# Spacing GpSimd's gathers and ranking a list-scheduled four-layer kernel anew

## The chip, the cores and the metric

The kernel runs on one core of a Trainium2 chip. A core has five engines that run beside each other, each with its own instruction queue in order: TensorE (PE, matmuls; its weight loads are listed as PEld), VectorE (DVE), ScalarE (ACT), GpSimd (POOL) and SyncE (SP, which here only issues DMAs). They meet through semaphores. The metric is the device time of one execution in microseconds (us): the median over the runs.

## What is computed

The input x is 8 sequences of 256 tokens with 128 features, in fp32. Four layers follow, each with a cross-attention to a context of 8 x 64 tokens and a feed-forward part, both added to x with a learned gate tanh(g):

```
for l in 0..3:
    x = x + tanh(g_xattn[l]) * xattn_l(layernorm(x), ctx)
    x = x + tanh(g_ffn[l])   * ffn_l(layernorm(x))
```

What bears on the change:

- Layer 0's feed-forward part is a mixture of experts: a base expert for every token, and for each token the two best of eight experts (128 -> 2 x 352 -> 128, SiLU gate), weighted by their softmax scores.
- Layer 1 has an attention of 16 heads over own tokens and context, and a dense mixture of eight small experts. Layer 2 has an attention of 16 heads over context, and a mixture of attention and feed-forward experts, gated by cosine similarities (the small tensors sims and sgate).
- Layer 3's feed-forward part quantises its weights to three values, w_q = clip(round(W / s), -1, 1) * s with s the mean of |W| of a row, and uses W + (w_q - W). It has one shared expert and the single best of eight experts for each token (128 -> 256 -> 128).

## The kernel before

**Tiles and stages.** The 2,048 tokens are 16 tiles of 128, in four chunks of four. x stays in SBUF. Matmuls run in fp32; "ps" in the profile is any PSUM bank, and rA, rC, rG, rK, rU and rF are regions of SBUF that many tiles share.

**The two routed mixtures.** Layer 0 and layer 3 send tokens to experts through DRAM. The normalised tokens are stored (xkd, zd), the routing makes index lists (d0idx, d30idx, d31idx), and each expert tile of 128 tokens is fetched by an indirect DMA that GpSimd issues (`gather`, L1151). PE transposes it (L888), multiplies it with its expert's weights (layer 0: L1263, L1282, L1288; layer 3: L2217, L2233, with L888 between), an evacuation copies it out of PSUM (L1301, L2245) and SP stores two tiles at a time (ygd by L1302, yd by L2246). Then the tokens fetch their experts' rows back, again by `gather` (index lists d0rows, d30rows, d31rows), and DVE adds them to x (L1312, L2252). There are 117 gathers: 39 of xkd, 32 of ygd, 19 and 11 of zd (layer 3 routes its first three chunks, then its last one), 12 and 4 of yd. SP stores the output two tiles at a time after L2252 (L2254).

**Other lines that the text touches.** `base_expert` (L1228, L1234) and `l3_shared` (L2193, L2197) are matmuls without routing, used as filler. L1512 are the scores of layer 1's attention, whose row maxima DVE takes (L1490); their operands come through a DMA rU<-rC (L1465, L1466) after L1458 and L1461. L1798 to L1805 prepare layer 2's gating from sims and sgate; L1800 is its matmul on PE, L1804 a step on ACT and L1805 one on DVE. L1826 is a matmul of layer 2's gating. L868 is the power function of the norms, on GpSimd. `l3_quantised` (L2120 to L2137) quantises two weight tensors in thirds: DVE makes two comparisons (L2129, L2130) and GpSimd four elementwise steps over 768 columns (L2131 to L2134).

**What sets the order.** The program isn't written in its order of execution. Each operation is recorded as a `Node` with a modelled cost and latency, its dependencies and a rank; `Plan.schedule` is a list scheduler over the five queues. At each step it takes, for each engine, the ready nodes that could start within a small slack of the earliest, and of these the one with the lowest rank; `emit` then writes each engine's instructions by planned start. The ranks come from the table RANKS: pairs of a node number and a rank, valid up to the next pair.

```
for (first, rank), (end, _) in zip(RANKS, RANKS[1:] + [(len(nodes), 0)]):
    for n in nodes[first:end]:
        n.rank = (rank, n.seq)
```

Where the plan has PE active for too small a share of the last 3.4 us (WINDOW, ENOUGH, LEAST), `fill` puts in dummy matmuls (bf16, 128x512, listed at L2298), whose results nobody reads. 31 small loads of constants for the later layers (L754, L993 to L1010, held back by `plan.hold`) are issued by SP among the stores of ygd. A gather is modelled at 1,250 ns of GpSimd and 1,300 ns more until it has landed.

Of the kernel before, what the change touches and what calls it, by code (L numbers as in the profile page):

```python
# [14 lines left out]
BF16 = mybir.dt.bfloat16  # L15
AF = mybir.ActivationFunctionType
ALU = mybir.AluOpType
AX = mybir.AxisListType

P = 128  # L20
# [67 lines left out]
class Node:  # L88
    __slots__ = (
        "seq", "rank", "calls", "cost", "lat", "deps", "kids", "wait", "ready", "table", "allocs", "uses", "line",  # L90
        "start", "eng", "end", "outs", "act",
    )


# [1 line left out]
SEM = 60.0  # L96


class Plan:
# [52 lines left out]
    def add(self, calls, items, cost, lat):  # L152
        n = Node()
# [15 lines left out]
        n.line = self.line()  # L169
        n.ready, n.start = self.hold, None  # L170
        n.act = sum(i[7] for i in items)
        n.outs = [x for i in items for x in i[1] if eng != "PE" and not isinstance(x, View)]
        for _, writes, reads, *_ in items:
            for x in reads:
# [67 lines left out]
    def schedule(self, square):  # L242
# [120 lines left out]
                    best = (t2, t, i)  # L363
            return best and best[1:]

        order = []
        todo = len(nodes)
        while todo:
            pick = None
            for e in ENGINES:  # L370
# [6 lines left out]
                for n in pool:  # L377
                    t = n.ready if n.ready > t0 else t0
                    if n.allocs:
                        ok, taken = True, []  # L380
                        for b in n.allocs:
                            pl = place(b, taken)
                            if pl is None:
                                ok = False
                                break
                            taken += range(pl[1], pl[1] + b.n)
                            if pl[0] > t:
                                t = pl[0]
                        if not ok:
                            continue  # L390
                    if e == "ACT" and n.table and n.table != table:
                        t += switch
                        if t - n.ready < PATIENCE:
                            t += 0.5 * switch
                    cand.append((t, n))
                    if t < low:
                        low = t
# [37 lines left out]
            for b in n.allocs:  # L435
                t1, i = place(b)
                t = max(t, t1)
                b.place = i
                kinds[b.kind] = kinds.get(b.kind, 0) + 1
                for j in range(i, i + b.n):  # L440
                    held[j] = b
                    spans[j].append([t, 1e18])
            n.eng, n.start = e, t
            free[e] = t + n.cost[e]
            lat = n.lat[e]
# [9 lines left out]
            else:  # L455
                x = next((x for x in n.outs if whole(x)), None)
                if x is not None:
                    heapq.heappush(steps, (n.end + SEM, n.seq, x))
                if begin is None and any(x.tensor.name == square.tensor.name for x in n.outs) and n.rank[1] > first_square:
                    begin = n.end + SEM  # L460
# [17 lines left out]
        order.sort(key=lambda n: (n.start, n.seq))  # L478
        self.order = order
        return order  # L480

    def dummy(self, j, weights, src):
        dst = self.psum[:, j * BANK : (j + 1) * BANK]
# [19 lines left out]


RANKS = [
    (0, -8.81423), (24, -3.9207), (39, 6.38523), (63, 5.89215), (87, 7.63505), (111, 8.13897), (135, 3.08915),
    (159, 5.79217), (183, 6.34169), (195, 2.37592), (219, 9.35483), (226, 7.73129), (239, 8.47319), (263, 9.41623),
    (287, 9.81073), (311, 9.81017), (335, 5.75831), (359, 7.11937), (383, 4.51516), (400, 12.473), (424, 11.4516),
    (448, 12.1111), (468, 10.9153), (492, 11.2491), (516, 13.9731), (527, 6.24473), (551, 4.81591), (575, 7.74998),
    (599, 9.83805), (623, 10.6955), (647, 5.78046), (671, 8.27812), (695, 4.60363), (719, -8.92199), (743, 3.38467),  # L510
    (767, 6.96523), (791, 3.62384), (815, 8.51202), (839, 1.56555), (863, 3.79945), (887, 6.97792), (911, 4.33277),
    (935, 8.78708), (943, 15.012), (951, 18.2171), (959, 16.913), (967, 10.4794), (975, 16.9253), (983, 9.99517),
    (991, 1.54625), (1015, 5.87219), (1039, 2.6703), (1063, -8.68786), (1087, 3.14673), (1096, 2.80187),
    (1120, 12.4378), (1144, 12.1551), (1153, 5.7225), (1177, 15.0894), (1183, 3.58836), (1193, 3.96122),
    (1217, 7.19124), (1241, 9.01458), (1250, 7.91182), (1274, 6.93102), (1280, 3.99039), (1290, 10.8385),
    (1314, 6.31445), (1338, 6.65857), (1354, 8.48851), (1378, 6.31126), (1402, 7.9314), (1411, 5.32165),
    (1435, 15.3732), (1441, -9.12596), (1451, -3.81797), (1475, -3.69121), (1499, 10.91), (1508, 15.3376),
    (1532, 13.6412), (1538, 9.82436), (1548, 4.51756), (1572, -4.85316), (1596, 11.2096), (1612, -3.99823),
    (1636, -3.026), (1660, 7.32202), (1669, 7.95703), (1693, 3.94619), (1699, 4.59663), (1709, 3.44889),
    (1733, 6.59853), (1757, 3.60586), (1766, 7.56498), (1790, 7.68471), (1796, 4.3326), (1806, 4.34554),  # L520
    (1830, 7.2283), (1854, 6.25525), (1870, 6.2584), (1894, 3.02858), (1918, 5.98574), (1937, 0.60987),
    (1961, 5.27954), (1982, 7.71269), (2006, 6.25101), (2030, 6.28834), (2046, 3.90444), (2070, 7.80619),
    (2094, 3.7545), (2118, 7.69472), (2142, 2.38528), (2145, 5.92942), (2169, 14.3495), (2193, 12.8278),
    (2208, 9.51468), (2232, 7.76875), (2256, -5.45801), (2271, 7.76656), (2295, 3.46247), (2319, 11.5164),
    (2334, 3.67181), (2358, -3.29604), (2382, 10.5902), (2397, 7.49049), (2421, 4.17373), (2445, 3.04442),
    (2460, -4.97886), (2484, -5.98313), (2508, 8.79012), (2523, 10.2729), (2547, -3.86213), (2571, 9.48064),
    (2586, 2.69215), (2610, 17.1353), (2634, 7.61745), (2649, -8.8357), (2655, 9.73474), (2676, 5.59728),
    (2700, 5.47862), (2707, 13.687), (2731, 10.4051), (2755, 10.1074), (2779, 7.67358), (2782, 4.52856),
    (2806, 5.49354), (2830, -9.18087), (2844, 8.0594), (2868, 8.15882), (2892, -9.18314), (2906, 7.30903),
    (2930, 3.85602), (2954, 4.00223), (2968, 4.2028), (2992, 12.5164), (3016, 15.0752), (3030, 9.25522),  # L530
    (3054, -9.20446), (3078, -3.75919), (3079, 5.5021), (3103, -8.64894), (3127, 5.41648), (3128, -9.10233),
    (3145, -9.09852), (3169, 10.0369), (3193, 3.34345), (3202, 6.24005), (3226, 4.85186), (3250, 3.79496),
    (3251, 3.12274), (3268, 2.65504), (3292, 5.52079), (3316, 8.04174), (3325, 6.36822), (3349, 12.6744),
    (3359, 17.8309), (3376, -8.71613), (3400, 14.6489), (3424, 6.97596), (3433, 7.31619), (3457, 1.40941),
    (3467, 1.92845), (3491, 10.0564), (3501, 6.76292), (3525, -4.75416), (3549, 3.12448), (3551, 2.78523),
    (3575, 1.25688), (3599, 5.04665), (3601, 14.9022), (3625, 11.1661), (3649, 6.38291), (3651, 11.7678),
    (3675, 7.02337), (3699, 4.12325), (3723, 10.4855), (3747, 14.702), (3762, 10.4015), (3786, 9.45812),
    (3810, 9.48594), (3811, 4.91636), (3828, 1.98819), (3852, 6.07668), (3876, 5.16349), (3885, 7.16907),
    (3909, 4.32541), (3919, 1.29563), (3943, 4.76685), (3967, 5.94095), (3969, 4.27357), (3993, 5.06055),
    (4017, 10.113), (4035, 10.3702), (4059, 17.4385), (4071, 8.68884), (4095, 17.3361), (4119, 4.54227),  # L540
    (4143, 8.44501), (4167, 6.73715), (4191, 7.19744), (4215, 7.46141), (4225, 7.86594), (4249, 9.71193),
    (4273, 8.26746), (4297, 12.837), (4315, -3.41036), (4339, 3.89787), (4345, 5.15199),
]


WINDOW, DUMMY, GUARD, ENOUGH, LEAST = 3400.0, 216.0, 150.0, 0.62, 0.48


def whole(x):
# [60 lines left out]
class Engine:  # L610
# [5 lines left out]
    def __getattr__(self, name):  # L616
        plan, eng = self.plan, self.eng

        def call(*args, **kw):
# [16 lines left out]
            elif eng == "POOL":  # L636
                c, lat = cost_pool(name, allargs, out, ins), 100.0
                if name == "indirect_dma_start":
                    c, lat = 1250.0, 1300.0
                    ins = [x for x in (kw["in_"],) if is_ap(x)]  # L640
                    for k in ("in_offset", "out_offset"):
                        if kw.get(k) is not None:
# [65 lines left out]
def tile_flamingo(ctx: ExitStack, tc: tile.TileContext, a: dict, out: bass.AP, n_sub: int = 8):  # L708
# [9 lines left out]
    def mk(shape, name, dtype=F32):  # L718
        return const.tile(shape, dtype, tag=name, name=name)

    regions = {k: mk([P, n], "r" + k) for k, n in (("A", 9792), ("G", 8192), ("U", 8192), ("K", 6144), ("C", 8960), ("F", 2048))}

    def put(region, at, shape, n=1):
# [1391 lines left out]
    def l3_quantised():  # L2115
        for i, (groups, size) in enumerate(((18, D), (9, 2 * D))):
# [9 lines left out]
            for k in range(3):  # L2126
# [1 line left out]
                q, lo = (z.rearrange("p (r l) -> p r l", l=size) for z in (bq_, bl_))  # L2128
                v.tensor_tensor(q, w[:, r], over(th[:, 0, r], size), ALU.is_gt)  # L2129
                v.tensor_tensor(lo, w[:, r], over(th[:, 1, r], size), ALU.is_lt)  # L2130
                g.tensor_tensor(q, q, lo, ALU.subtract)  # L2131
                g.tensor_tensor(q, q, over(sc[:, r], size), ALU.mult)
                g.tensor_tensor(q, q, w[:, r], ALU.subtract)
                g.tensor_tensor(q, q, w[:, r], ALU.add)  # L2134
                qf = bq_.rearrange("p (n l) -> p n l", l=P)
                for k3 in range(2):
                    evac(w3t[:, i, 6 * k + 3 * k3 : 6 * k + 3 * k3 + 3, :], turned(qf[:, 3 * k3 : 3 * k3 + 3], 3))  # L2137
# [234 lines left out]
```

## Time and profile before

| | us |
|---|---|
| median of 9 runs | 969.83 |
| lowest and highest | 968.21 and 973.93 |
| the profiled execution | 973.31 |
| its span in the trace | 971.1 |
| PE, DVE, ACT, POOL busy | 913.7, 684.6, 382.6, 299.0 |

A row of the profile's groups names line, engine, operation, output<-input and count; behind the first bar stand the busy time and the mean ns of one, behind the second the engine's idle time ahead of these instructions and what ended it ("<-DVE rstd L865" is a wait for DVE's result of line 865; "issue" is a wait that the profile can't name). The granted clock (PEclk) is the share of TensorE's full speed: 1 or 0.5 at any moment of this trace, means over a stretch lie between.

### The profile page before, as it was taken

How to read it: one execution, taken by the hardware profiler on the slowest of the kernel's cores; microseconds unless marked ns; L12 is line 12 of the kernel's file. 1: busy time of each engine (PE TensorE's matmuls, PEld its weight loads, DVE VectorE, ACT ScalarE, POOL GpSimd, SP SyncE). 2: the span in 40 equal slices, each digit the busy share in tenths (PEclk: the TensorE clock that was granted, in tenths of full speed). 3: DMA queues.
4: the chain of work that ended last, by engine and by line, in shares of the span. 5: the costliest groups of instructions: out<-in, count | busy, mean ns of one | idle time of the engine just before them, and what ended most of it. 6: DMA issues, size and time to landing. Idle time of an engine off the chain costs nothing. (4 is left out here: it accounts for less than half of the span.)

```text
span 971.1 us, 18385 instructions
## 1 busy us (share of the span) xinstructions
PE 913.7 (94%) x6669; PEld 613.0 (63%) x6669; DVE 684.6 (70%) x2059; ACT 382.6 (39%) x1096; POOL 299.0 (31%) x320
## 2 busy tenths in 40 slices
PE   8999799999999999999999899989999999999983
PEld 4646587755554464455677677557775768867872
DVE  7885355569776766774866799867579768697642
ACT  2242223214445436346756877101134044044631
POOL 6406530266110010101311234330125741213464
PEclk9999999979999999999999999989999999999997
DMA  8412421121000000000102000210000000000353
GB/s 267 131 54 72 104 45 36 37 66 35 19 15 10 14 10 10 11 2 23 45 1 72 1 18 23 52 25 1 1 2 0 2 1 12 12 12 20 67 87 90
DMA packets 55781, 36.50 MB, mean 38 GB/s; under 512 B 14898, under 2 KB 52027, under 8 KB 55692
## 3 DMA queue, kind: packets, MB, share of 16 engines
q1 hardware_dynamic: 47724, 25.56, 9.4%
q0 software_dynamic: 3744, 7.68, 4.2%
q10 hardware_dynamic: 4224, 2.10, 0.7%
q8 instruction: 54, 0.88, 0.4%
q14 instruction: 35, 0.29, 0.1%
HBM read 25.08 MB, written 7.67 MB: 34 GB/s over the span
## 5 line engine op out<-in xcount | busy, mean ns | idle before, releaser
L868 POOL TENSOR_TENSOR rstd<-rstd,mhalf 128x4 f32<-128x4 f32 (+2 forms) x44 | 44.5, 1013 | 298.5 <-DVE rstd L865 256.5
L1490 DVE TENSOR_REDUCE nmx<-ps 128x2 f32<-128x640 f32 x128 | 100.2, 818 | 17.6 <-PE ps L1512 16.3
L1512 PE MATMUL ps<-rU 32*128 32x256 f32 (+1 forms) x1024 | 104.9, 445 | 5.1 <-DMA rU<-rC 2.1
L1521 ACT ACTIVATE rA<-ps 128x1024 f32<-128x1024 f32 x64 | 65.1, 1023 | 75.3 <-PE ps L1512 71.6
L1909 PE MATMUL ps<-rK,rG 128*128 128x128 f32 x768 | 90.3, 276 | 0.0
L1909 PEld LDWEIGHTS ps<-rK,rG 128*128 128x128 f32 x768 | 88.0, 192 | 3.3 <-issue 2.8
L1512 PEld LDWEIGHTS ps<-rU 32*128 32x128 f32 (+1 forms) x1024 | 56.4, 187 | 48.8 <-DVE nmx L1490 22.4
L1736 ACT ACTIVATE rA<-ps,nm 128x64 f32<-128x64 f32 x256 | 75.9, 348 | 10.2 <-DVE nm L1732 7.8
L1901 PE MATMUL ps<-rG,rK 128*128 128x512 f32 x128 | 60.8, 624 | 0.0
L1736 ACT ACTIVATION_READ_ACCUMULATOR rA<-ps,nm 128x1 f32 x256 | 60.7, 242 | 0.0
L1263 PE MATMUL ps<-rA,rC 128*128 x156 | 52.6, 467 | 0.0
L1151 POOL DMA_INDIRECT rC<-xkd,d0idx x39 | 37.3, 955 | 35.0 <-PE ps L888 21.0
L1901 PEld LDWEIGHTS ps<-rG,rK 128*128 128x128 f32 x128 | 25.1, 203 | 27.8 <-issue 27.0
L1895 DVE TENSOR_TENSOR rG<-rC,ps 128x512 f32<-128x512 f32 x64 | 40.4, 678 | 0.0
L1557 PE MATMUL ps<-rA 128*9 128x256 f32 (+1 forms) x512 | 37.0, 385 | 0.5 <-ACT rA L1521 0.4
L1151 POOL DMA_INDIRECT rC<-ygd,d0rows x32 | 31.7, 992 | 13.8 <-issue 7.2
L1263 PEld LDWEIGHTS ps<-rA,rC 128*128 128x128 f32 x156 | 27.6, 194 | 10.4 <-ACT rC L1258 0.5
L1288 PEld LDWEIGHTS ps<-rA,rU 128*128 128x128 f32 (+1 forms) x234 | 30.4, 195 | 3.4
L1721 PE MATMUL ps<-rG,rA 128*128 128x512 f32 x64 | 31.1, 604 | 1.0 <-DVE rA L1753 0.6
L1758 PE MATMUL ps<-rU,rA 128*128 128x128 f32 x256 | 31.9, 278 | 0.0
L1288 PE MATMUL ps<-rA,rU 128*128 (+1 forms) x234 | 31.8, 279 | 0.0
L1758 PEld LDWEIGHTS ps<-rU,rA 128*128 128x128 f32 x256 | 30.1, 192 | 2.1 <-issue 1.3
(523 smaller groups left out, 2062.2 us busy)
## 6 DMA issues: line engine op xcount, KB each, us to landing
rA<-in_L_ffn_exp_wgu_dram SPq DMA_DIRECT2D x4, 704.0 KB
ygd<-rC SPq DMA_DIRECT2D x19, 128.0 KB
rK<-in_L_xattn_Wkv_dram SPq DMA_DIRECT2D x2, 1024.0 KB
rU<-rC SPq DMA_DIRECT2D x64, 32.0 KB
yd<-rG SPq DMA_DIRECT2D x14, 128.0 KB
x<-in_x_dram SPq DMA_DIRECT2D x4, 256.0 KB
rA<-in_L_ffn_exp_wd_dram SPq DMA_DIRECT2D x2, 512.0 KB
xkd<-rC ACTq DMA_DIRECT2D x4, 256.0 KB
```

The lines of the kernel that those rows point to most:

```text
L868: power(r[:, 0 : n * len(kinds)], n * len(kinds))
L1151: g.indirect_dma_start(out=dst, out_offset=None, in_=src, in_offset=bass.IndirectOffsetOnAxis(ap=idx, axis=0))
L1263: with together():
L1288: with together():
L1490: v.tensor_reduce(nmx_of[b][:, qt, h0 : h0 + 2], sc[:, :, 0:KEYS], AX.X, ALU.max, negate=True)
L1512: with together(cost=640.0 if bm is not None else 500.0):
L1521: s.activation(e, st, AF.Exp)
L1736: with together():
L1758: with together(cost=2280.0):
L1895: v.tensor_tensor(xe[:, 2 * i + k, :], src, pgs[:, k, :], ALU.mult)
L1901: with together():
L1909: with together():
```

## The change

Three edits.

First, a gather node is marked, and the scheduler lets a gather start only 5,000 ns (in the plan's time) after the third-last one. If it was held up by that, `after` puts a tiny copy ahead of it on GpSimd: it copies one column of the newest finished result of an engine other than GpSimd (as the plan sees it) into a scratch column, so that at run time GpSimd waits for that step before it issues the gather.

```
+        n.gather = n.lat.get("POOL") == GATHER
...
+                    if n.gather and len(gathers) > 2 and gathers[-3] + GATHERS > t:
+                        t = gathers[-3] + GATHERS
...
+            if n.gather:
+                if len(gathers) > 2 and gathers[-3] + GATHERS >= t and ended:
+                    self.after(n, max((c for c in ended if c[0] <= t), default=None))
+                gathers.append(t)
...
+                    if e != "POOL":
+                        ended.append((n.end + SEM, n.seq, x))
...
+    def after(self, n, mark):
+
+        if mark is None:
+            return
+        x = mark[2]
+        while len(x.shape) > 2:
+            x = x[:, 0]
+        x, dst = x[:, 0:1], self.scratch
+        if x.dtype == BF16:
+            dst = dst.bitcast(BF16)[:, 0:1]
+        n.calls["POOL"].insert(0, lambda e, fix: e.tensor_copy(dst, x))
...
+GATHER, GATHERS = 1300.0, 5000.0
```

Second, the four GpSimd steps of the quantisation work on halves of each group of columns, in a loop over the halves:

```
-                g.tensor_tensor(q, q, lo, ALU.subtract)
-                g.tensor_tensor(q, q, over(sc[:, r], size), ALU.mult)
-                g.tensor_tensor(q, q, w[:, r], ALU.subtract)
-                g.tensor_tensor(q, q, w[:, r], ALU.add)
+                for h in (slice(0, size // 2), slice(size // 2, size)):
+                    qh, wh = q[:, :, h], w[:, r, h]
+                    g.tensor_tensor(qh, qh, lo[:, :, h], ALU.subtract)
+                    g.tensor_tensor(qh, qh, over(sc[:, r], size // 2), ALU.mult)
+                    g.tensor_tensor(qh, qh, wh, ALU.subtract)
+                    g.tensor_tensor(qh, qh, wh, ALU.add)
```

Third, the table RANKS is replaced as a whole: ranges of up to 24 nodes become ranges of up to 16, and nearly every value differs.

```
 RANKS = [
-    (0, -8.81423), (24, -3.9207), (39, 6.38523), (63, 5.89215), (87, 7.63505), (111, 8.13897), (135, 3.08915),
...
+    (0, -10.4081), (16, -5.43032), (24, -10.1179), (39, -4.23222), (55, -3.9187), (63, 1.22023), (79, 15.8053),
...
```

Counted in the instruction orders of the two programs: PE's real matmuls are the same in number and shape, in another order, and its dummies are 125 before and 123 after. GpSimd has 87 tiny copies and 24 halves more. 14 PSUM evacuations of 128x256 go from DVE to ACT. SP issues the same 276 DMAs, in another order: eight of the constants (sims, one sgate, layer 2's norms) come first among them, and the stores of the output come earlier among those of yd.

## The prediction

> **What bounds the kernel now.** I read the page's busy times and its slices first, to see which engine sets the pace.
>
> ```profile
> PE 913.7 (94%) x6669; PEld 613.0 (63%) x6669; DVE 684.6 (70%) x2059; ACT 382.6 (39%) x1096; POOL 299.0 (31%) x320
> ...
> PE   8999799999999999999999899989999999999983
> ...
> PEclk9999999979999999999999999989999999999997
> ```
>
> TensorE (PE) sets it: 913.7 of 971.1 us busy, so all its idle time together is 57.4 us. GpSimd (POOL), on which every part of the change sits, is busy for 299.0 us. It can cost time only where PE waits for it. Next I read a table by stage.
>
> ```profile
> 0.00:27.00 27.00, 23.74 (x103) 12.90 (x103) 21.48 (x99) 6.55 (x15) 15.86 (x29) 0.94 0.89 273
> ...
> 100.00:125.00 25.00, 17.67 (x94) 13.86 (x93) 9.02 (x28) 5.26 (x14) 11.86 (x14) 0.88 0.41 95
> ...
> 200.00:225.00 25.00, 22.88 (x111) 12.20 (x110) 18.54 (x38) 3.44 (x11) 13.74 (x15) 0.80 0.22 57
> ...
> 930.00:971.10 41.10, 23.25 (x139) 18.58 (x137) 13.31 (x35) 9.31 (x24) 19.98 (x21) 0.81 0.45 92
> ```
>
> The columns are the stretch, its length, busy us (and instructions) of PE, weight loads, DVE, ACT and POOL, then the granted clock and the DMAs. Subtract PE's busy time from the length: 3.3 us of idle time lie in the first stretch, 7.3 in 100 to 125, 2.1 in 200 to 225, 17.9 in the last one. Together that is 30.6 of the 57.4; the rest is strewn in waits below 1.5 us, except one of 3.3 us at 603. So the change can be worth much only in three places: the stall near 115, the entry into the first attention near 205, and the tail.
>
> **Part 1: PE's own work.** The instruction orders of the two programs hold the same real matmuls; the planned dummies (L2298) go from 125 to 123. One takes 0.38 us, so -0.7 us. They also move: 24 to 50 in layer 1's attention, 31 to 18 in layer 2, 70 to 55 elsewhere. Moved at equal number they cost nothing by themselves. That the planner wants as many as before also says that it sees about as much room on PE as before.
>
> **Part 2: the stall near 115.** The waits of PE in 100 to 125 are one line.
>
> ```profile
> PE ps L1800 <- DVE tk_simsq L1798: 7.3, 1, 7.3
> ```
>
> Behind it lies SyncE's queue: 31 small loads of constants are issued from 106.14 to 122.4, about 0.5 us each, behind the fourth store of ygd, which waits for its tile. The 25th (the second sgate) is seen by ACT's L1804 at 123.49, 17.4 us after the first issue. The new order puts sims and seven more loads first, but DVE now meets this block two tiles earlier, and still passes through L1805, which needs the 25th load. Counting PE's rows, the fourth ygd store is ready 2.7 us later, and PE reaches the block 6.2 us later. The stall would run from 114.1 + 6.2 = 120.3 to 123.5 + 2.7 + 0.5 (ACT, DVE) = 126.7: 6.4 us in place of 7.3, so I take -0.9. Bounds: -7.3 (gone) and +2.7 (all of the later store).
>
> **Part 3: the entry into the first attention.** Here 32 gathers of ygd follow the last store of ygd; four of them, two norms and a transfer rU<-rC lead to the first scores (L1512).
>
> ```profile
> 206.00 0.81 PE L1512 MATMUL ps<-rU 29*128 29x320 f32 x4 [2.12 <-DMA rU<-rC]
> ...
> 209.95 4.87 PE L1512 MATMUL ps<-rU 29*128 29x320 f32 x20
> ...
> 218.71 1.70 PE L1512 MATMUL ps<-rU 29*128 29x320 f32 x12
> ```
>
> Two things are to be seen: PE waited 2.12 us for the chain, and afterwards the same matmul took 244 ns (4.87 over 20) where it later took 142. The granted clock was 0.5 from 207 to 217. Pricing the slow rows against their fast forms gives 2.0 (L1512), 1.1 (L1458 and L1461, 2.28 against 1.18) and 1.1 (L1228, 2.08 against 1.02): 4.2 us in all. In the new order only three gathers go at once; the fourth waits for a DVE step behind the first. PE's filler before L1512 is equal, some 21 us, so the delay is seen. One pitch of a gather is 1.25 us (0.95 and 0.30 between two): +1.3, bounds 0 (the filler hides it) and +4 (a landing of 2.5 us and 1.5 of DVE come between). The slow clock I leave as it is, since the wait ahead of it does not shrink.
>
> The Trainium skill, "TensorE: Matmul & The Clock Gate", Part 1: The HAM clock gate, says that the clock falls to half after an idle window of about 3.4 us. Here 2.12 us of idle time was followed by 0.5, so the row is stricter than the rule. By the rule the stretch could vanish with slightly denser work and the sum would be 4.2 us lower; by the row it stays.
>
> **Part 4: paced gathers and tiny copies.**
>
> ```profile
> L1151 POOL DMA_INDIRECT rC<-xkd,d0idx x39 | 37.3, 955 | 35.0 <-PE ps L888 21.0 <-issue 4.9 <-DVE d0idx L1139 4.5
> ...
> L2133 POOL TENSOR_TENSOR rA<-rA,rU 128x768 f32<-128x768 f32 x6 | 12.8, 2138 | 0.5
> ...
> L1974 POOL COPY rU<-caus 128x128 f32<-128x128 f32 x2 | 0.7, 341 | 0.1
> ...
> L1634 POOL MEMSET rC<- 128x4 f32 x2 | 0.2, 106 | 0.1
> ```
>
> 87 of the 117 gathers get a copy of one column ahead of them that waits for a step of DVE or ACT. No row shows that copy: it lies between the memset of 0.106 and the copy of 0.341, so 9 to 30 us of POOL in all; I take 0.15 (nearest to the memset, since its width is one column). POOL's 672 us of idle time hide it. What the wait itself costs depends on how much PE work lies between a gather's release and the matmul that reads it. A gather needs 0.3 + 2.9 from its start to landing and the copy and handoffs some 0.5, or 3.7 to 4.2 us. Counting PE's rows in both orders, the smallest such reserve before is 5.9 us; after it is 4.0, 4.6, 4.7, 5.4 and 5.9 for the five tightest. So the waits hide, barely. Beyond the gathers, PE's waits with under 1 us of PE work in front of them rise from 72 to 85, those under 1.5 fall from 214 to 212. The strewn 27 us of idle time over 214 such waits is 0.13 each; 13 sharper ones make 1.7 at twice that. I take +1.0 for both, bounds -2 and +5. Queued behind a waiting copy on POOL are the pow steps (L868, 1.05 us) whose norms DVE awaits; that is where an excess would go.
>
> **Part 5: quantisation in halves.** The four POOL steps of a third take 1.8, 1.6, 2.1 and 1.9 us over 768 columns. Halved, 24 more instructions come in; at 0.1 (memset) to 0.3 (the copy) each, 2.4 to 7 us of POOL. In 700 to 830 PE waited only 2.4 us, none of it for these steps; DVE and PE's other work hide them. 0, bounds -1 and +2; without the cover it would be the 2.4 to 7.
>
> **Part 6: the tail.** The chain that ended last, and the gathers' landings from the DMA view of 900 to 971:
>
> ```profile
> 954.23 3.36 DMA yd<-rG
> ...
> 957.66 3.28 issue
> 960.94 0.95 POOL rG L1151
> ...
> 964.71 2.94 DMA rG<-yd,d31rows
> ```
> ```profile
> rG<-yd,d30rows POOLq DMA_INDIRECT x12, 2.5
> rG<-zd,d31idx POOLq DMA_INDIRECT x11, 5.4
> ```
>
> After the last store of yd four gathers go 1.25 us apart. Then comes 2.94 us to landing, one DVE step and the store of the output. Two things change. First, the last four gathers become five, the fourth waiting for the sum that reads the first, the fifth for the second's: first start plus 1.4 + 2.94 + 0.35 + 0.4 makes 5.1 us for the last start against 3.77, so +1.3. Second, L2197 (shared expert, 1.98 us), which ran after the last L2233, is now ahead of it but for a quarter; the last yd tile ends PE's work, 1.8 us later against PE's end. Sum +3.1. Bounds: -4.8, if the spacing brings zd's landings from 5.4 toward 2.5 and removes PE's 2.9 us of waits there (L2217, L888) and the 1.9 that DVE waited too long for yd's stores (L2245 waited 4.4); +5, if also the pauses show.
>
> **The sum.** -0.7 - 0.9 + 1.3 + 1.0 + 0 + 3.1 = +3.8 us, against the profiled run's 973.31 (span 971.1 and 2.2 around it), or 977.1. That run stands 3.5 us above the median of the nine runs, 969.83; the median after is then **973.6**. A measurement of this kernel can tell about 0.3% (2.9 us) from no change.
>
> **The rivals.**
> - Faster: the new order carries a denser first attention (26 more dummies there, nine among its first scores), the clock holds, -4.2; spacing relieves the tail, -4.8 in place of +1.8 for the later tile; the end's +1.3 stays. 969.8 - 0.7 - 0.9 + 0 - 4.2 - 4.8 + 1.3 = about 960.5. For it: 5.4 us landings of the eleven gathers in a row, and the 0.80 clock. Against it: the wait ahead of that stretch is not shorter.
> - Slower, beyond 980: the pauses bind. In the last layer 30 gathers of zd wait in pairs for steps that themselves follow an earlier tile's transposes. It decides once the real landing is above the 4.0 us reserve; then each of 15 pairs is late by about 0.5 to 1.4 (5.4 less 4.0): 7.5 to 21 us, I take 11 for half of them at the longer price and more, and the total is about 985. Against it: only two reserves of the 30 there are under 5 us.
> - It does little: POOL already waited 21.0 us for L888 in layer 0's gathers, so those were spaced; and the rest cancels. 969.8.
>
> **How the numbers follow.** The forecast, 0.45 (966 to 980, within it 0.34 slower, 0.08 same, 0.03 faster); faster rival, 0.34; binding pauses, 0.15, slower; little, 0.06, same 0.05 and faster 0.01. Faster 0.38, same 0.13, slower 0.49. The unknown bounds add to -16 and +15 about the median; leaving a tenth on either side gives 956 to 988. The forecast's own range is 966 to 980.
>
> **What would show it.** Right: the last yd gather starts over 4.5 us after the first; PE's last L2233 is its end; a PE wait of 6 to 7 us near 120; clock 0.5 after the first L1512; PE busy 913. Wrong: no half clock near 210, zd d31 landings near 2.5 with the tail's PE idle under 14 us (faster), or PE waits at L888 for zd above 5 us in all (slower). A change of PE's idle time in layers 1 and 2 by more than 5 us would break the sum where I had least to go on.

## The result and the profile after

The changed kernel takes **1001.12 us** (median of 20 runs, 995.22 to 1008.74) against 973.14 for the kernel before in the same series (62 runs): a ratio of 1.0295 [1.0274, 1.0316]. It is slower by 28 us where the forecast had +3.8, and above the forecast's range. The profiled execution took 997.99 us with a span of 996.2, so the span grew by 25.1. The first rows of the page, in the same places as those shown of before:

```profile
PE 912.3 (92%) x6667; PEld 616.5 (62%) x6667; DVE 690.9 (69%) x2060; ACT 383.5 (38%) x1098; POOL 320.9 (32%) x431
...
PE   8999789978999999999999999879899999999881
...
PEclk9999989999999999999999999979899999999996
```

PE's own work is unchanged (912.3 us, before 913.7). So all of the 25.1 us is time in which PE stands: 20.7 us more before its last matmul (42.0 to 62.7), 5.8 more behind it (15.4 to 21.2), less 1.4 of busy time. The slices show new dips at 9 and 10 and at 26 to 29, and a longer one at the end. In the file after, lines stand 49 to 51 further down (L888 is L937, L1151 is L1200, L1512 is L1561, L1854 is L1903, L2233 is L2284). The waits of PE over the whole span, in us in total, number and longest:

```profile
PE ps L937 <- DVE rA L1903: 14.3, 3, 10.5
PE ps L1561 <- DVE nmx L1539: 7.0, 11, 1.8
PE ps L1337 <- DVE rU L1335: 5.6, 1, 5.6
PE ps L1561 <- DMA rU<-rC: 2.9, 2, 1.5
PE ps L1849 <- DVE tk_simsq L1847: 2.9, 1, 2.9
PE ps L937 <- DMA rG<-zd,d31idx: 1.8, 2, 1.6
```

Before, the longest wait of all was the 7.3 us near 115. PE's idle time by stage, summed from its matmuls in both traces:

| PE's idle time, us | before | after | |
|---|---|---|---|
| start to layer 2's gating product (L1800) | 12.7 | 9.3 | -3.4 |
| from there to the last L1263 | 0.0 | 5.6 | +5.6 |
| to the first score of layer 1 (L1512) | 2.1 | 4.3 | +2.2 |
| first quarter of these scores | 1.5 | 6.9 | +5.4 |
| rest of layer 1, first part of layer 2 | 12.5 | 11.5 | -1.0 |
| layer 2, first L1884 to a quarter of L1909 | 4.5 | 16.2 | **+11.7** |
| to layer 3's last L2084 | 5.1 | 2.5 | -2.6 |
| tail, to PE's end | 3.6 | 6.4 | +2.8 |
| behind PE's end | 15.4 | 21.2 | **+5.8** |

**The largest piece, layer 2.** Rows of PE, DVE, POOL and SP between 619 and 655, start and duration first:

```profile
622.87 10.98 SPq L2104 DMA_DIRECT2D rU<-in_ctx_dram  x16
633.89 0.60 SPq L2160 DMA_DIRECT2D rU<-in_L_ffn_expert_w_dram  x1
```
```profile
638.15 2.67 DVE L2171 TENSOR_REDUCE bq_s<-rU 128x6 f32<-128x768 f32 x3 [6.42 <-DMA rU<-in_L_ffn_expert_w_dram]
...
644.42 0.68 DVE L1086 TENSOR_TENSOR tk_t<-tk_next,tk_m 128x32 f32<-128x32 f32 x1
...
645.14 0.19 DVE L1087 TENSOR_TENSOR tk_t<-tk_t,eidx 128x32 f32<-128x32 f32 x1
```
```profile
643.95 1.10 POOL L2182 TENSOR_TENSOR rA<-rA 128x384 f32<-128x384 f32 x1 [17.37 <-DVE rA L2179]
```
```profile
654.00 2.39 PE L937 MATMUL ps<-ident,rA 128*128 128x128 f32 x10 [10.52 <-DVE rA L1903]
```

Read upwards. PE stands 10.5 us for L1903, the third split of layer 2's gating weights (each split writes one of three bf16 parts of them). That chain runs on DVE from 644 to 653.8. It stands behind the reductions of the quantisation (L2171), for which DVE waited 6.4 us, because SP issues 16 small context loads (11 us) ahead of the last expert weights. Before, DVE waited 5.7 us in the same place, but behind it PE had other work and stood 3.3:

```profile
636.81 0.95 DVE L2122 TENSOR_REDUCE bq_s<-rU 128x6 f32<-128x768 f32 x1 [5.68 <-DMA rU<-in_L_ffn_expert_w_dram]
```
```profile
639.56 0.36 PE L1826 MATMUL ps<-simn,rC 128*128 128x8 f32 x2 [3.26 <-DVE rC L1823]
```

Beside the chain lie the new order's first quantisation steps.

**The tail**, POOL's rows at the end:

```profile
981.30 0.98 POOL L1200 DMA_INDIRECT rG<-yd,d31rows  x1 [0.65 <-issue]
982.29 0.19 POOL L1200 COPY after<-x 128x1 f32<-128x1 f32 x1
985.00 0.99 POOL L1200 DMA_INDIRECT rG<-yd,d31rows  x1 [2.52 <-issue]
...
990.11 0.98 POOL L1200 DMA_INDIRECT rG<-yd,d30rows  x1 [0.21 <-issue]
```
```profile
rG<-zd,d31idx POOLq DMA_INDIRECT x11, 3.2
```

The last five gathers begin over 8.8 us (before, four over 3.8), and each has a copy of 0.19 us ahead of it. The eleven zd gathers land in 3.2 us instead of 5.4 (the trace pairs four of them with their issue, before only one), but PE's waits for them (3.3 us together) do not go away.

### The profile page after: what moved, and what is told of

Read it like the earlier page. It is cut to its first block, busy times and chain, and to the rows that moved or that the text cites. A ratio compares the mean times of both kernels' runs of the same rounds, so it can differ in the third digit from the quotient of the medians.

```text
span 996.2 us, 18581 instructions
## 1 busy us (share of the span) xinstructions
PE 912.3 (92%) x6667; PEld 616.5 (62%) x6667; DVE 690.9 (69%) x2060; ACT 383.5 (38%) x1098; POOL 320.9 (32%) x431
## 4 chain that ended last, share of the span: by engine, by line
PE 61%; DVE 16%; DMA 8%; issue 5%; POOL 4%; SPq 3%; ACT 2%; POOLq 0%; DVEq 0%; ACTq 0%
PE ps L1958 7%; PE ps L1561 7%; PE ps L1312 4%; PE ps L1606 4%; PE ps L937 4%; DVE nmx L1539 3%; PE ps L2011 2%; PE ps L1337 2%; PE ps L1807 2%; PE ps L1770 2%; PE ps L2349 2%; DMA rC<-ygd,d0rows 1%; DMA rG<-yd,d30rows 1%; PE ps L1453 1%; PE ps L1733 1%
## 5 line engine op out<-in xcount | busy, mean ns | idle before, releaser
L1561 PE MATMUL ps<-rU 29*128 29x320 f32 (+1 forms) x1024 | 104.6, 442 | 11.4 <-DVE nmx L1539 7.0
L1958 PE MATMUL ps<-rK,rG 128*128 128x128 f32 x768 | 91.6, 278 | 0.0
L1561 PEld LDWEIGHTS ps<-rU 29*128 29x128 f32 (+1 forms) x1024 | 55.0, 184 | 52.0 <-DVE nmx L1539 29.0
L1785 ACT ACTIVATE rA<-ps,nm 128x64 f32<-128x64 f32 x256 | 76.3, 350 | 14.3 <-DVE nm L1781 11.8
L1950 PE MATMUL ps<-rG,rK 128*128 128x512 f32 x128 | 58.1, 607 | 0.0
L1312 PE MATMUL ps<-rA,rC 128*128 x156 | 54.6, 479 | 0.6 <-issue 0.6
L1200 POOL DMA_INDIRECT rC<-xkd,d0idx x39 | 38.3, 982 | 20.3 <-issue 7.9
L1337 PEld LDWEIGHTS ps<-rA,rU 128*128 128x128 f32 (+1 forms) x234 | 31.9, 198 | 11.7 <-DVE rU L1335 6.1
L1337 PE MATMUL ps<-rA,rU 128*128 (+1 forms) x234 | 33.7, 283 | 6.0 <-DVE rU L1335 5.6
L1200 POOL DMA_INDIRECT rC<-ygd,d0rows x32 | 32.1, 1004 | 13.3 <-issue 8.8
L937 PE MATMUL ps<-ident,rC 128*128 128x128 f32 x159 | 30.8, 295 | 4.1 <-DVE rC L933 1.7
L1329 DVE TENSOR_TENSOR rC<-rC,ps 128x352 f32<-128x352 f32 x39 | 20.2, 517 | 19.5 <-PE ps L1312 17.9
```

The lines of the kernel that those rows point to most:

```text
L937: with together(cost=110.0 * n + 105.0):
L1200: g.indirect_dma_start(out=dst, out_offset=None, in_=src, in_offset=bass.IndirectOffsetOnAxis(ap=idx, axis=0))
L1312: with together():
L1337: with together():
L1561: with together(cost=640.0 if bm is not None else 500.0):
L1785: with together():
```

## The experiments

Ratios are to the kernel before, run on the same chip, with 95% intervals. The kernel before took 971 to 973 us on three chips of this study and 1017 to 1018.5 on the two others; what that does is told in the third and fifth group. In the fences below, lines stand up to 25 further down again.

**1. Each edit alone, or left out.** Theory B of the first four expectations: the pauses bind; theory A: the new ranks.

Run e1, without the pauses (limit and copies), with the new ranks and halves:

```
-                    if n.gather and len(gathers) > 2 and gathers[-3] + GATHERS > t:
-                        t = gathers[-3] + GATHERS
-                if len(gathers) > 2 and gathers[-3] + GATHERS >= t and ended:
-                    self.after(n, max((c for c in ended if c[0] <= t), default=None))
```


> The new ranks and the halves, without the limit of three gathers in 5 us and without the tiny copies. Theory A (the new order loses: DVE meets the reductions of layer 3's weights before the gating of layer 2, and the tail's last tile is late): stays slow, 990 to 1000 us, with the PE wait of about 10 us for L1903 near 650 still there. Theory B (the pauses lose): falls to 968 to 976, about the kernel before.

Measured: 1.0383 [1.0318, 1.0449]. The planner fits the same ranks into another plan, with 167 dummies, 42 of them in the tail (from 928 us on); PE's wait for the split stays (10.6 longest).

Run e2, the pauses alone, on the old ranks and whole quantisation steps (the diff's first edit, without the other two):


> The limit and the tiny copies with the old ranks and whole quantisation steps. Theory A: 970 to 978, some us over the kernel before for the pauses at the entry of layer 1 and in the tail. Theory B: 990 or more.

Measured: 1.0426 [1.0357, 1.0496], 181 dummies. So neither ranks nor limit alone is better than both together. e1's time lies above both theories' ranges, e2's fits B; neither run isolates the price of an edit, because the scheduler makes a new plan of some 18,500 instructions each time.

Run e3, the halves alone, ranks and pauses as before, each second half ranked as its first:


> Old ranks, no pauses, only the quantisation in halves (each second half takes its first half's rank). Both theories: within 0.4% of the kernel before (969 to 977), since PE never waits for these steps for long. If halves matter by themselves, over 980.

Measured: 1.0117 [1.0036, 1.0198], with PE waiting 3.9 us for the split. Here too the plan shifted.

Run e4, the changed plan without its copies; the limit stays. The trace after holds 90 copies, not 87: GpSimd has 111 instructions more, but three normalisations (L884; L933 in the file after) have left it.

```
-                if len(gathers) > 2 and gathers[-3] + GATHERS >= t and ended:
-                    self.after(n, max((c for c in ended if c[0] <= t), default=None))
```


> The changed kernel with the limit kept in the planner but without the 87 copies, so GpSimd's order is planned with spaces and nothing holds the gathers at run time. Theory A: 988 to 1000, the copies are worth at most 8 us, in the tail (5.8 us after PE's end) and at the entry of layer 1. Theory B, if it is the waits and not the spacing: 968 to 980.

Measured: 1.0198 [1.0133, 1.0262]; behind PE's end 16.8 us instead of 21.2, the split's wait still 10.6. Every other instruction keeps its place, so this edit is clean: with copies 1.03, without 1.02, so they make about a third of the excess, and the rest is in the plan (ranks and limit).

**2. Where in the order, and which copies.** The loads at L2104 (before: L2055) are issued behind the last weights load, in the changed kernel (f1) and in the kernel before (f2), with nothing else moved:

```
+        last = max(i for i, n in enumerate(order) if n.seq in self.keys)
+        held = [n for n in order[:last] if n.seq in self.late]
...
+        order = [n for n in order[: last + 1] if n.seq not in self.late] + held + order[last + 1 :]
```


> The changed kernel, with SyncE's 16 small context loads for layer 3 (11 us of its queue) issued after the last load of layer 3's expert weights in place of ahead of it; nothing else moves. Theory A (DVE's reductions of these weights wait for the load in order, and the gating of layer 2 stands behind them): DVE's wait of 6.4 us goes, PE's 10.5 us wait near 643 to 654 shrinks to 4 or less, time 990 to 994, 8 to 11 us under the changed kernel. Theory B (the gating chain is late by its own length): no change, 998 to 1003.

> The kernel before with the same move of SyncE's 16 loads. Theory A: DVE's 5.7 us wait goes, and with it PE's wait of 3.3 us near 636: 3 to 5 us faster than before, 966 to 969. Theory B: no change.

Measured: 1.0239 [1.0164, 1.0315] and 0.9897 [0.9803, 0.9992]. DVE's wait is gone in both. In the changed kernel the stretch from the first L1884 to a quarter of L1909 falls from 115.5 to 109.7 us, and the longest wait for the split from 10.5 to 4.0. The whole time (998.0 us) doesn't settle f1: its interval holds the changed kernel's 1.0295. In the kernel before PE's 3.3 us go, and the time is 1% lower, by an interval that just leaves out no change; two further runs with this move (g2, h2) stand at 0.986 and 0.989.

Run f3, no copies ahead of layer 3's gathers; those of layer 0 stay:

```
-                if len(gathers) > 2 and gathers[-3] + GATHERS >= t and ended:
+                if len(gathers) > 2 and gathers[-3] + GATHERS >= t and ended and len(gathers) < 71:
```


> The changed kernel without the tiny copies ahead of layer 3's gathers (46 gathers), those of layer 0 stay; the plan is the same. Theory A (the copies hurt where the plan is short, in layer 3): 988 to 993, nearly all of what leaving out all 87 gave. Theory B (copies cost alike everywhere, by their number): half of it, about 995.

Measured: 1.0192 [1.0115, 1.0270]; from the last L2084 to the last L2217 45.0 us (after 51.6, before 47.4), behind PE's end 15.7 (21.2, 15.4). So as far as the intervals of f3 and e4 can tell, what the copies cost, they cost in layer 3.

Run f4, POOL's steps whole again, in the place of the second half:

```
+                    for m, (x2, op) in zip(plan.nodes[first:], whole_ops):
+                        m.calls["POOL"] = [] if h.start == 0 else [
+                            lambda e, fix, q=q, x2=x2, op=op: e.tensor_tensor(q, q, x2, op)
+                        ]
```


> The changed kernel in the same planned order, but the quantisation's POOL steps emitted whole, each in the place of its second half, nothing in that of the first. If halves cost by themselves (as the kernel before with halves, 10.8 us over, suggests): 3 to 8 us faster than the changed kernel, 993 to 998. If it was the order that moved there: within 2 us of it.

Measured: 1.0336 [1.0259, 1.0412], the split's wait 11.7. In the new order the halves do no harm that shows; in the trace the stretch from the first L1884 to a quarter of L1909 takes 118.1 us with whole steps, 115.5 with halves.

**3. Another chip.** The same three ideas combined or refined: the changed kernel with f1's and f3's edits (g1), the kernel before with f2's edit and eleven constants issued first (g2), the kernel before in its own order with halves (g3), and the changed kernel with the quantisation moved behind the third split (g4). These four met a chip on which the kernel before took 1017.01 us.


> The changed kernel with the context loads behind the weights and without the copies ahead of layer 3's gathers. If the two are independent, the sum of both: 1001 less 3 to 6 less 7 to 10, 986 to 991. If either hides the other, 993 or more.

> The kernel before with the context loads behind the weights, and among the 31 constants those that DVE meets at the stall near 115 issued first (b_proj, nkv, ln scale and bias, sims, sgate: 11 loads, some 5.5 us of issue from 106.1). If the stall is the SyncE queue as the prediction said: PE's 7.3 us wait falls under 1, and the half clock after it (6.8 us) goes: 952 to 957, 7 to 11 us under the move of the loads alone (963.4). If something else ends it: no change.

> The kernel before in its own order, each POOL step of the quantisation emitted as two halves one after the other in the same place. If halves let DVE's small steps through earlier (its waits end at the end of a GpSimd step, now 1.0 us long and not 1.8): 0 to 4 us faster than before. If the price is the extra instructions: 1 to 4 us slower. The 10.8 us that the planner's halves cost with old ranks would then be the order.

> The changed kernel, with all quantisation steps that stood ahead of the third split of layer 2's last gating before it (L1903) moved behind it on every engine; the rest of the order stays. Theory A (what makes the gating late is the quantisation beside and ahead of it: the wait for the weights, DVE's own comparisons, and DVE's small two-input steps that end only when a GpSimd step of 1 us ends): PE's waits for L1903 fall from 14.3 us to under 4, DVE's step of 128x32 goes back from 0.7 to 0.9 us to about 0.2, time 988 to 994. Theory B (the loads alone, worth what the move of the loads gave): 996 to 999.

Measured: 0.9977 [0.9951, 1.0002]; 0.9861 [0.9791, 0.9930]; 0.9985 [0.9953, 1.0017]; 0.9878 [0.9823, 0.9933]. The order before with halves (g3) can't be told from before: the halves by themselves cost nothing that shows. But its trace is 45 us longer than that shown of before, of which PE idles 10.3 more ahead of the first L1512, and the way from the last L2084 to the last L2217 takes 9.3 more: stretches with rows of gathers. And paced kernels were suddenly no slower than before. Either that chip is slower throughout, or rows of gathers are.

One pair of runs settles this: g2 and h2 (in the next group) are the same program on a chip of each kind, with spans of 998.8 and 954.2 us. From a quarter of layer 1's scores to the first L1884, where no row of gathers lies, g2 takes 327.9 us and h2 327.6. The difference sits in four stretches that hold rows: +10.2 up to L1800, +13.2 in the first quarter of the scores, +9.6 from a quarter of L1909 to the last L2084, +14.8 from there to PE's end. So that chip isn't slower throughout. A row of g3's DVE beside gathers of zd:

```profile
927.17 0.69 DVE L897 TENSOR_REDUCE m<-ps 128x8 f32<-128x512 f32 x1 [11.78 <-remote]
```

"remote" is a wait whose releaser the profile doesn't name.

In g4, meant to free the split's chain of the quantisation, PE now waited for the quantisation itself (12.4 us, L2185's counterpart).

**4. The changed kernel again, and the three pieces together**, on a chip where before takes 970.89: the changed kernel (h1), g2's program (h2), the changed kernel with loads, quantisation and layer 3's copies treated as in f1, g4 and f3 (h3), and the same with the copies kept (h4).


> The changed kernel as it is, once more, because the kernel before took 1017 us on the chip of the last four runs and 970 to 973 on the others. If gathers back to back slow the other engines on such a chip and the pauses avoid that, then there the ratio to before is 0.99 to 1.00 (1005 to 1017 us), with PE's idle time before the first score of layer 1 at 19 to 21 us against 23 to 25 of before's order. If that chip is slower by a share throughout, the ratio is 1.03 there as elsewhere (1047). On a chip where before takes 970 both say 1.025 to 1.032, 995 to 1003 us.

> The kernel before with the 16 small context loads behind the last expert weights, and eleven constants of the stall near 115 issued first. If the wait of DVE's reductions for SP's queue costs 6 to 9 us in either order, the ratio is 0.985 to 0.990 (957 to 963 where before takes 972). If the constants are worth something beside it, the stall of 7.3 us shrinks below 4 and the ratio is 0.980 to 0.985; if not, PE waits for something else in the same place and the ratio is that of the context loads alone, 0.990.

> The changed kernel with three edits together: context loads behind the last weights, the quantisation steps that stood ahead of the third split moved behind it, no copies ahead of layer 3's 46 gathers. If the excess sits in layer 2's gating and in the copies of layer 3, and the three pieces add up (4 + 2 + 8 of the 28 us), the ratio is 1.010 to 1.018 where before takes 970 (980 to 988 us). If the quantisation has only moved its wait from the split to the transposes behind it, the third piece is 0 and the ratio is 1.018 to 1.022.

> As the one before, with the copies ahead of layer 3's gathers kept. If the copies cost 6 to 9 us there on a chip where before takes 970, the ratio is 0.006 to 0.009 above the last one. If this run is on a chip where before takes 1010 or more and rows of gathers slow the other engines there, it is below the last one instead, by 5 us or more.

Measured: 1.0348 [1.0256, 1.0441]; 0.9890 [0.9804, 0.9976]; 1.0224 [1.0158, 1.0290]; 1.0344 [1.0266, 1.0423]. The copies of layer 3 are again worth 10 us (h3 against h4). With the copies kept, loads and quantisation together are worth nothing that shows (h4 against h1): PE's wait was handed on. PE's waits in h3 between 606 and 725:

```profile
PE ps L952 <- POOL rA L2206: 14.1, 2, 12.4
PE ps L952 <- DVE rA L1919: 3.5, 1, 3.5
```

In h2 the stall near 115 is gone from the trace (PE's idle time up to L1800 is 7.1 us, before 12.7), but its ratio is that of f2. The intervals are too wide to price it.

**5. The quantisation out of that stretch.** Every quantisation step, the reductions that wait for SP's loads with them, is put 80 us later in the order (and one constant step, L1167, that shares its space) in i1; i2 adds the two other pieces. In both, the moved steps no longer keep their order with others that use the same space, so some values are overwritten too early and the output isn't the reference's; every instruction still runs.

```
+        order.sort(key=lambda n: (n.start + SHIFT * (lo <= n.seq < hi or n.seq == 3764), n.seq))
...
+SHIFT = 80000.0
```


> The changed kernel with every quantisation step (of DVE, POOL, PE and ACT) put 80 us later in the order, at its old pitch, so about where the kernel before has most of them; one constant step of DVE that shares their space goes with them. If the early quantisation is what holds up layer 2's gating, the longest wait for the third split (10.5) falls below 4, the stretch from the first L1933 to a quarter of L1958, 115.5 us, to 103 to 107, and the ratio to 1.018 to 1.024. If the gating chain is late by itself in the new order, the stretch stays at 112 or above and the ratio at 1.028 or above.

> The same, with the 16 context loads behind the last weights load and no copies ahead of layer 3's gathers. If the three causes add, 1.002 to 1.010 (973 to 980 where before takes 971); if only the copies count, 1.018 to 1.024, as in the run that moved the quantisation only behind the third split.

Measured, on a chip where before takes 1018.5: 0.9937 [0.9911, 0.9962] and 1.0057 [1.0030, 1.0084]. The stretches of i1 from 640 on; length, then busy us of PE, weight loads, DVE, ACT, POOL, the granted clock and the DMAs:

```profile
640.00:660.00 20.00, 20.00 (x53) 9.35 (x52) 8.25 (x40) 2.28 (x7) 2.44 (x2) 1.00 0.16 33
660.00:706.00 46.00, 46.00 (x300) 35.60 (x299) 28.03 (x84) 6.25 (x22) 2.08 (x2) 1.00 0.00 1
706.00:730.00 24.00, 20.54 (x139) 18.43 (x139) 18.20 (x41) 0.85 (x2) 6.60 (x7) 0.86 0.00 1
730.00:760.00 30.00, 23.70 (x123) 14.15 (x121) 26.74 (x72) 11.01 (x21) 21.01 (x22) 0.94 0.00 1
760.00:786.00 26.00, 20.77 (x110) 12.71 (x107) 21.79 (x57) 7.04 (x13) 11.99 (x13) 0.87 0.00 1
```

The half of the expectation that names the stall is right, and further than it said: the 66 us from 640 to 706 hold no idle time at all, and the stretch to a quarter of L1909 takes 88.4 us instead of 115.5. But from 706 to 786, where the quantisation now runs, PE stands 15.0 us. To half of L1909 it is 167.1 us, after 166.8, before 156.7. So the early quantisation, its wait for SP's loads included, is what held up the gating there, and taking it elsewhere without a plan for it only moves the 15 us along. The ratios are on a chip of the other kind and don't test the expectations: that i2's lies in the range for three adding causes is chance.

In the tail, h3 differs from h4 by the copies alone, and i2 from i1 by the copies and the context loads, which are issued 300 us earlier. From the last L2084 to the last L2217, first h4 (copies) and h3 (none) where before takes 971, then i1 (copies) and i2 (none) where it takes 1018.5:

```profile
917.20:967.50 50.30, 43.59 (x277) 34.58 (x276) 26.52 (x95) 22.48 (x55) 31.16 (x51) 1.00 0.35 77
```
```profile
917.60:962.40 44.80, 42.59 (x276) 34.60 (x276) 26.68 (x95) 22.43 (x55) 27.23 (x29) 1.00 0.41 89
```
```profile
934.20:984.80 50.60, 43.26 (x276) 34.46 (x275) 26.54 (x95) 22.19 (x55) 30.96 (x51) 1.00 0.35 77
```
```profile
942.60:1005.60 63.00, 49.85 (x277) 40.41 (x276) 26.15 (x95) 22.47 (x54) 27.04 (x29) 0.85 0.31 63
```

With the copies, both chips take 50.3 to 50.6 us. Without them the one gains 5.5 and the other loses 12.4: PE idles 13.2 us instead of 7.3, and its clock drops to 0.85. Rows of i2's POOL, PE and DVE there:

```profile
973.04 0.94 POOL L1213 DMA_INDIRECT rG<-zd,d31idx  x1 [0.30 <-issue]
974.28 0.94 POOL L1213 DMA_INDIRECT rG<-zd,d31idx  x1 [0.30 <-issue]
```
```profile
977.24 0.42 DVE L2299 COPY rG<-ps 128x256 f32<-128x256 f32 x1 [3.78 <-remote]
```
```profile
977.72 1.22 PE L2300 MATMUL ps<-rA,rG 128*128 x4 [3.72 <-DVE rG L2299]
```

While gathers go 1.25 us apart, DVE stands 3.78 us on a "remote" wait, and PE stands behind DVE. In h3 the same eleven gathers, equally close, have no such wait. Over all traces, "remote" waits of more than 1 us stand in g1, g2, g3 and i2 alone: in g1 and i2 only beside layer 3's gathers, which have no copies there, and in none of the kernels with all copies (g4, i1). So on two of the five chips, rows of gathers hold up other engines, and a pause prevents it; on the others it only costs. The changed kernel itself wasn't run on a chip of the first kind; its two kin there (g4, i1) stood at 0.988 and 0.994 of before.

## Why the prediction was wrong

- **Part 1** (-0.7): right. 123 dummies, PE busy 1.4 us less.
- **Part 2** (-0.9, a stall of 6.4 near 120): the stall split in two. PE waits 2.9 at L1849 near 115, as sims now come early, and 5.6 at L1337 at 122: in order ahead of DVE's L1335 stand two steps that wait 3.5 and 2.9 us for the null keys and a norm's scale, later constants of the same queue. I followed the 25th load and not the others that DVE meets. The stages give +2.2 in place of -0.9.
- **Part 3** (+1.3): up to the first score +2.2 (a copy that reads a buffer holds PE's next writer 1.5 us at L1430; the transfer rU<-rC 2.9). Then +5.4 in the first quarter of the scores, where PE waits for DVE's row maxima: not in the working. The slow clock, left as it was, fell there from 10.2 to 3.4 us in the profiled run, so this stretch took 61.6 us in both. It was 10.2 again in h1 and f3, which take 64.2 and 63.9 us, and in e4, which takes 61.4 without copies. So some 2.5 us there may be the copies of layer 0; these are single profiles.
- **Part 4** (+1.0): mis-sized. A copy takes 0.19 us, near the 0.15 taken, but its pause costs 8 to 10 us in layer 3 (f3, h3 against h4). I looked at PE's reserve ahead of single gathers; the price lies in the chain of yd gathers at the end and in zd's pitch: the last eleven start over 21.0 us instead of 12.5 (15.2 in f3, without the copies). And there are 90 copies, not 87.
- **Part 5** (0): right for the steps, with two halves of 4.0 us against 7.4 for a whole third, and g3 shows no cost. Wrong in what went with it: the new ranks put GpSimd's steps of all six thirds between 644 and 723, where before one third lay at 643 to 649 and the other five between 733 and 789. I priced the step in the place it came from and not in the one it went to.
- **Part 6** (+3.1, of it 1.8 and 1.3): +2.8 ahead of PE's end and +5.8 behind it. The last start came 8.8 us after the first, not 5.1: the second of these gathers waits as well, 2.5 us that the profile can't name (2.3 in h4 in the same place).
- **The step that failed most** stands ahead of the six: "So the change can be worth much only in three places". It read the places off the idle time of the old order, and so put layer 2 at nothing, though new ranks can open a wait where there was none. The runs showed +11.7 us of idle time there, the largest piece of the 25.1: L1903's chain comes late behind the early quantisation and its wait for SP's loads (f1, i1). The sign was there: the wait of 3.3 us that the prediction put at 603 ends at 639.6, behind that same queue. Its last sentence did name layers 1 and 2 as where it "had least to go on". Only parts of this piece were undone without a price elsewhere, so how much of the 28 us it makes is not shown by a whole time; the copies' 8 to 10 us are.
- **The range.** The bounds of the six parts add to -19.6 and +14.2 about the sum, not to -16 and +15. The measured time lies above either.
- **The rivals.** "The pauses bind" was right in sign and named the copies, but not the place: zd's waits stay at 3.3 us, below its bound of 5. It would have given 985; by idle time, layer 2's stall makes up most of the rest. "Faster" got its zd landings (3.2 us) and no time from them.

## What to carry to other kernels

When an order is ranked anew, make the table of the bound engine's idle time for every stage of the new order, also where the diff changes nothing: list what stands ahead of each long chain on its engine, and what these steps wait for, down to the queue of small loads. A pause between DMAs is priced where the chain ends, not where there is slack. And an edit whose use depends on the chip (here the same copies save 12 us of the tail on one and cost 5 on another) has to be measured on several before it is kept.

## What the runs showed of the hardware

- **Rows of gathers.** On two of five chips gathers 1.25 us apart hold up DVE and ACT by up to 11.8 us at a time (g2, g3), and PE behind them; with pauses they don't. What differs between these chips no run tells: in those traces the landings of gathers aren't paired with their issues.
- **Small DVE steps beside GpSimd's.** A 128x32 step with two SBUF inputs takes 0.19 us (L1087), but 0.68 (L1086) while POOL's L2182 runs, and it ends when that ends: 645.10 against 645.05. Beside the whole steps of before, 1.8 us long, such steps took up to 1.76 (L1037), and a step with one input 1.84 (L1837). This agrees with the Trainium skill, "SBUF — State Buffer", section "Who interferes with whom": a DVE instruction with two SBUF inputs contends with a GpSimd instruction that reads SBUF. Shorter GpSimd steps may so help a gating chain (f4's longer wait); no run isolates this.
- **Slow clock.** The time at half clock up to PE's end was 37.5 us before and 47.8 after, yet PE's busy time did not grow. h1 is the changed kernel itself, and its profile has 17 us of half clock from 15 to 32 that the profile after lacks; its first L1263 starts at 91.6 us against 85.5. So some 6 us of a single profile can be the clock and not the change, and a piece below that, read from one profile, isn't safe.
